# Third block of a four-block network on one Trainium2 core: normalization, rows and gate logits of two tiles placed directly behind the recurrence's work on them, with own room for the gate's matrix

## The chip, the core and the metric

The kernel runs on one core of a Trainium2 chip. A core has a matrix engine (PE, with its weight loads shown as PEld), a vector engine (DVE), an activation engine (ACT), GpSimd (POOL) and a sync engine (SP), which here does nothing but issue DMA transfers. Each engine works through its own queue in order, and they meet through semaphores. SBUF is the working memory with 128 partitions; PSUM is where PE writes and from which DVE and ACT read. The metric is device time in microseconds of one call, the median over runs; before the change it is 2966.4 us (three runs, 2960.71 to 2970.5).

## The reference

A residual stream x of 16 sequences of 64 tokens, 256 wide (1024 tokens, held as 8 tiles of 128 tokens), passes four blocks of cross-attention, a mixing layer and a feed-forward layer. The change touches the third block ("L2"): its linear recurrence and the routed experts behind it.

```python
x = x + _L2_xattn_ref(_layernorm(x), ctx_768, ...)          # 8 heads of 64 over 1024 keys
x = x + _L2_attn_ref(_layernorm(x), theta_log, nu_log, gamma_log, B_re, B_im, C_re, C_im, D)
x = x + _L2_ffn_ref(_layernorm(x), Wg, bg, W1, W2, W3)

def _L2_attn_ref(x, ...):                 # a complex linear recurrence along each sequence
    Bu = einsum('hd,bld->blh', B_norm, x)
    _, h = associative_scan(_binop, (Lam, Bu), axis=1)
    return einsum('oh,blh->blo', C, h).real + D * x

def _L2_ffn_ref(x, Wg, bg, W1, W2, W3):   # T = 1024 tokens, E = 8 experts, 2 of them per token
    gate_logits = xt @ Wg + bg
    top_v, top_i = top_k(gate_logits, 2)
    expert_label = one_hot(top_i, E).sum(axis=1)
    seq = cumsum(expert_label, axis=0) * expert_label
    valid = (seq > 0) & (seq <= 160)      # the first 160 tokens of each expert
    ...                                   # gather the rows of each expert
    h = silu(disp @ W1) * (disp @ W2)
    out = h @ W3
    ...                                   # weighted sum of a token's two outputs
```

The place of a token among those of its expert is a running sum over all 1024 tokens, so routing needs the logits of every tile.

## The kernel before

The layers run one after the other. `L2_xattn_attn` (line 1680) runs the cross-attention `heads64` (line 420) and the recurrence together: PE's order in it is the order in which the program text issues (a "manual schedule"), and the other engines are ordered by a scheduler.

`heads64` goes in 32 steps, four to a tile of 128 tokens. A step holds 13 us or more of PE work: transposes of the softmax of the step before (`keys_first`, L235), averages over keys (`misc<-ctx,pT`, from helper line 69), scores (L507), and every fourth step the output product (24 matmuls from L69). Between these it calls `breathe(0)` to `breathe(3)`; `breathe` is the recurrence's `go` (line 1800), which does nothing at place 3 and otherwise runs one piece of the current chunk. A chunk is two tiles, `chunk(k)` at line 1744, a generator cut in pieces by `yield`. Chunk k may start when the attention has finished tiles 2k and 2k+1 (`more`, line 1810). The pieces are, in order:

1. layer normalization of the two tiles on DVE and POOL into `os`;
2. four PE transposes of `os`, two evictions to `hTs` (one on DVE, one on ACT), and the D term on POOL;
3. eight matmul records into PSUM, scaled into `bu` on ACT;
4. products with cosine and sine and two scans on DVE and POOL; an empty piece follows;
5. eight matmul records back to 256 columns, added to the residual stream `xs` by DVE (L89).

So chunks 0, 1 and 2 run inside the attention's steps. Chunk 3 can start only after the last tile, when the attention has ended, and runs alone: `while lru.go(): pass`.

Then `L2_ffn` (line 1396) starts. `norm_x` (line 184) normalizes all eight tiles into `htok` (L170), transposes each (L179) and evicts to `hT` (lines 62 and 64, DVE and ACT in turn). `keep_row` (L1090) issues one DMA per tile, which writes the normalized rows to `hs` in HBM, from where experts gather them. `gate_logits` (line 1010) makes, for each tile, two matmuls with the gate's matrix and one with its bias row (the profile has two records for each matmul and one for each transpose): 128 x 8 outputs. DVE copies all logits to `lg` (L1404), and `route` (line 1092) computes top two, places and the table of tokens, on DVE with small matmuls. The gather of the first expert's rows (L1327, POOL's queue) waits for its result, `tokens` (L1411). Then eight experts run on PE.

Weights go through a ring of two slots; a "pack" takes a slot when its user two packs earlier is done, and one pack is loaded ahead. The gate's matrix and bias are a pack of their own (`pack_L2_gate`), between the recurrence's pack and expert 0's. PSUM tiles named `misc` come from two buffers in turn, so a third user waits for the eviction of the first. The tile `past` (line 1268) belongs to the block routing of the first and second block.

Of the kernel before, what the change touches and what calls it, by code (L numbers as in the profile page):

```python
# [11 lines left out]
F32 = mybir.dt.float32  # L12
# [3 lines left out]
ALU = mybir.AluOpType  # L16
# [3 lines left out]
B, S, D = 16, 64, 256  # L20
T = B * S
NT = T // 128
# [3 lines left out]
E = 8  # L26
# [16 lines left out]
class Net:  # L43
# [1208 lines left out]
    def block_experts(self, r, n_blocks, later=False):  # L1252

        nc = self.nc
        ps = self.misc([128, E])
# [9 lines left out]
        nc.vector.tensor_copy(n, end[:1, E - 1 :])  # L1265
        self.n_blocks = nc.values_load(n, min_val=0, max_val=n_blocks, skip_runtime_bounds_check_because="counted")
        shape = [128, n_blocks, E]
        past = self.lp.tile(shape, F32, name="past")
        nc.vector.tensor_tensor(
            past, self.steps[:, :n_blocks].unsqueeze(2).to_broadcast(shape),  # L1270
            end.unsqueeze(1).to_broadcast(shape), ALU.is_ge,
# [16 lines left out]
        ps = self.misc([128, n_blocks])  # L1288
# [14 lines left out]
        for m, to in zip(r.masks, r.at):  # L1303
            t = self.gate("back_t")
            nc.vector.tensor_tensor(t, r.place, first.unsqueeze(1).to_broadcast([128, NT, E]), ALU.add)
            nc.vector.tensor_tensor(t, t, m, ALU.mult)
            slot, _ = self.over_experts(t, ALU.add, "back_r")
# [75 lines left out]

        self.some_blocks(block, L1_FEW, L1_BLOCKS)

    def pack_L2_gate(self):
        self.slot()
        return self.load("L2f_Wg"), self.load_row("L2f_bg")

    def pack_L2_expert(self, e):  # L1390
        self.slot()
        return self.load("L2f_W1", e), self.load("L2f_W2", e), self.load("L2f_W3", e)
# [2 lines left out]

    def L2_ffn(self):
        nc = self.nc
        gw, gb = self.pack()
        self.norm_x()
        self.routed = r = self.route_setup(2)  # L1400
        for i in range(NT):
            self.keep_row(i)
        lg = self.gate("lg")
        nc.vector.tensor_copy(lg, self.gate_logits(gw, gb))  # L1404
        for _ in self.route(r, lg, 0, among_chosen=True):
            pass
        ps = self.misc([128, E, 2])
        cols = self.ident[:S, :S].rearrange("p (e n) -> p e n", e=E)[:, :, :2]
# [7 lines left out]
        for k, m in enumerate(r.masks):  # L1416
            t = self.gate("l2_t")
            nc.vector.tensor_tensor(t, late, m, ALU.mult)
            out, _ = self.over_experts(t, ALU.add, f"l2_late{k}")
            nc.vector.tensor_tensor(t, r.place, first.unsqueeze(1).to_broadcast([128, NT, E]), ALU.add)  # L1420
            nc.vector.tensor_tensor(t, t, m, ALU.mult)
            slot, _ = self.over_experts(t, ALU.add, f"l2_slot{k}")
# [6 lines left out]
        for e in range(E):  # L1429
# [10 lines left out]
            for v, (s0, n) in enumerate(L2_CUTS):  # L1440
                hb = self.lp.tile([n, D], F32, tag=f"hb{n}", bufs=2, name="hb")
                self.gather_rows(hb, self.hs, tokens[:n, e, v : v + 1])
                ps = self.misc([128, 2, 128])
# [4 lines left out]
            for m in range(8):  # L1448
                ps = self.lps.tile([128, 2, CAP], F32, tag="gu", bufs=2, name="gu")
# [7 lines left out]
            ps = self.lps.tile([128, 2, CAP], F32, tag="o", bufs=2, name="po")  # L1457
# [232 lines left out]
    def recurrence(self):  # L1690
        nc = self.nc
# [19 lines left out]
        def wrapped(x, n, name):  # L1711

            k = self.lp.tile([128, n], F32, name=f"{name}_k")
            nc.vector.tensor_scalar(k, x, 1.0 / two_pi, 12582912.0, ALU.mult, ALU.add)
            nc.vector.tensor_scalar(k, k, 12582912.0, None, ALU.subtract)
            y = self.lp.tile([128, n], F32, name=f"{name}_y")
            nc.vector.scalar_tensor_tensor(y, k, -hi, x, ALU.mult, ALU.add)
            nc.vector.scalar_tensor_tensor(y, k, -mid, y, ALU.mult, ALU.add)
            nc.vector.scalar_tensor_tensor(y, k, -lo, y, ALU.mult, ALU.add)
            nc.vector.tensor_scalar(y, y, PI_DOWN, -PI_DOWN, ALU.min, ALU.max)  # L1720
            return y

        phi = wrapped(theta, 1, "phi")
        ang = self.lp.tile([128, S], F32, name="ang")
        nc.vector.tensor_scalar(ang, self.steps, phi, None, ALU.mult)
# [15 lines left out]
        def flat(x):  # L1741
            return x.rearrange("p b s -> p (b s)")

        def chunk(k):
# [4 lines left out]
            for t in range(2):  # L1749
                x = self.xs[:, 2 * k + t, :]  # L1750
                mv, rs = self.norm_tile(x, 1e-5)
# [3 lines left out]
            hT = self.lp.tile([128, 2, CHUNK], F32, tag="hTs", name="hTs")  # L1755
            for t in range(2):
                self.evict(hT[:, :, t * 128 : (t + 1) * 128], self.transposed(os[t]))
                x = self.xs[:, 2 * k + t, :]
# [5 lines left out]
            for n, m in enumerate((br, bi)):  # L1764
                ps = self.misc([128, CHUNK])
# [27 lines left out]
            for t in range(2):  # L1793
                po = self.misc([128, D])
                at = slice(t * 128, (t + 1) * 128)
                self.mm(po, [(flat(hr)[:, at], cr), (flat(hn)[:, at], ci)])
                self.add_to_x(2 * k + t, po)
            yield

        def go(place=0):  # L1800
            if place == 3:
                return
            if s.work is None and s.next < NC and s.ready >= 2 * s.next + 2:
                s.work = chunk(s.next)
                s.next += 1
            if s.work is not None and next(s.work, s) is s:
                s.work = None
            return s.work is not None or s.next < NC
# [391 lines left out]
    def run(self, layers):  # L2200
        tc, nc, a = self.tc, self.nc, self.a
# [4 lines left out]
            "L1_attn": (self.L1_attn, [self.pack_L1_attn, self.pack_L1_boom]),  # L2206
            "L1_ffn": (self.L1_ffn, []),
            "L2_xattn_attn": (self.L2_xattn_attn, [lambda: self.pack_heads64("L2"), self.pack_L2_attn]),
            "L2_ffn": (self.L2_ffn, [self.pack_L2_gate] + [lambda e=e: self.pack_L2_expert(e) for e in range(E)]),
            "L3": (None, [lambda: self.pack_heads64("L3"), self.pack_L3_attn, self.pack_L3_ffn]),  # L2210
        }
        self.packs = [p for l in layers for p in plan[l][1]]
# [187 lines left out]
```

## Time and profile before

| what | value |
|---|---|
| median of three runs | 2966.4 us (2960.71 to 2970.5) |
| the profiled execution | 2962.24 us |
| span of its core in the profile | 2960.5 us |
| mean granted PE clock | 0.949 of full |
| PE / DVE / ACT busy share of the span | 91% / 49% / 35% |
| attention and recurrence of the third block, up to the last output product | ends at 1813.1 us |
| chunk 3 alone, to its last addition to `xs` | 1813.1 to 1830.6 us |
| transposes and gate matmuls of `L2_ffn` | 1830.7 to 1847.8 us |
| routing up to `tokens` | 1847.8 to 1864.6 us |
| first expert matmul | 1869.5 us |

The profiled execution took 2962.24 us, of which 2960.5 us are the span; the remaining 1.7 us lie around it. Rows of the timeline give the start, the duration, the engine, the line, the operation with output and inputs, the count of merged instructions, and in brackets the idle time before them and what ended it. The table of stretches gives, for each stretch, busy time and instruction count of PE, PEld, DVE, ACT and POOL, the granted PE clock as a share of full, the DMA share and the GB/s.

### The profile page before, as it was taken

What the parts mean: (1) busy time and instruction counts of PE and PEld (TensorE: products, weight loads), DVE (VectorE), ACT (ScalarE), POOL (GpSimd) and SP (SyncE); (2) the same over time, 40 slices, a digit from 0 to 9 for tenths busy, and PEclk for the clock granted to TensorE, in tenths of its full rate; (3) what the DMA queues carried; (4) which work ended last, traced back from release to release, by engine and by line L of the source; (5) the groups of instructions that cost most, each with busy time, mean ns of one, the idle gap of its engine ahead of it and who ended that gap; (6) DMA issues with size and microseconds to landing.
All of it is one profiled execution on the core that took longest, in us unless ns stands there. A gap on an engine that the chain in (4) does not pass through costs nothing. (4 is left out here: it accounts for less than half of the span.)

```text
span 2960.5 us, 42845 instructions
## 1 busy us (share of the span) xinstructions
PE 2687.8 (91%) x16972; PEld 1979.6 (67%) x16972; DVE 1462.2 (49%) x3117; ACT 1045.9 (35%) x2353; POOL 302.6 (10%) x407
## 2 busy tenths in 40 slices
PE   7887997999999898989999997899998898897899
PEld 3566784666666687857776776886766566665678
DVE  3655114666666643234444344324436656658581
ACT  2322122555555431223332331122335455455330
POOL 1111223000000112310101011201001000000000
PEclk9987998999999997989999997899999999998999
DMA  9603772110100115802111112551123122121210
GB/s 237 180 34 119 267 248 70 31 37 26 37 26 23 40 36 186 277 22 66 45 45 56 54 43 93 217 195 45 47 61 92 51 79 67 48 68 54 60 34 8
DMA packets 79222, 253.57 MB, mean 86 GB/s; under 512 B 15151, under 2 KB 26955, under 8 KB 69291
## 3 DMA queue, kind: packets, MB, share of 16 engines
q1 hardware_dynamic: 59562, 165.01, 18.0%
q0 software_dynamic: 13312, 80.28, 8.0%
q10 hardware_dynamic: 6144, 5.51, 0.5%
q8 instruction: 135, 2.21, 0.3%
q14 instruction: 69, 0.56, 0.1%
HBM read 233.80 MB, written 14.82 MB: 84 GB/s over the span
## 5 line engine op out<-in xcount | busy, mean ns | idle before, releaser
L223 DVE TENSOR_REDUCE nmx<-sc 128x1 f32<-128x1024 f32 x264 | 311.7, 1218 | 226.7 <-PE sc L507 135.2
L225 ACT ACTIVATE p<-sc,nmx 128x1024 f32<-128x1024 f32 x264 | 294.6, 1116 | 315.2 <-DVE nmx L223 314.5
L507 PE MATMUL sc<-ctxT,qp 128*128 128x512 f32 (+1 forms) x1024 | 357.7, 604 | 0.0
L507 PEld LDWEIGHTS sc<-ctxT,qp 128*128 128x128 f32 (+1 forms) x1024 | 139.5, 190 | 155.2 <-issue 153.0
L69 PE MATMUL halves<-ctx,pT 128*128 128x192 f32 x1024 | 191.0, 343 | 9.4 <-DVE xs L89 4.0
L69 PEld LDWEIGHTS halves<-ctx,pT 128*128 128x128 f32 x1024 | 178.3, 203 | 12.3 <-DVE xs L89 4.5
L69 PE MATMUL misc<-ctx,pT 128*128 128x192 f32 x1024 | 177.6, 327 | 0.5 <-DVE qT L472 0.5
L235 PE MATMUL ps_t<-ident,p 128*128 128x128 f32 x1088 | 146.8, 277 | 25.3 <-ACT p L225 17.6
L69 PEld LDWEIGHTS misc<-ctx,pT 128*128 128x128 f32 x1024 | 166.3, 191 | 2.2 <-DVE qT L472 1.0
L2010 ACT ACTIVATE da<-rep,al 128x252 f32<-128x252 f32 x256 | 114.7, 498 | 114.8 <-DVE x L2020 95.3
L237 ACT COPY pT<-ps_t 128x512 f32<-128x512 f32 x182 | 104.3, 585 | 139.3 <-PE ps_t L235 137.2
L235 PEld LDWEIGHTS ps_t<-ident,p 128*128 128x128 f32 x1088 | 126.7, 142 | 39.2 <-ACT p L225 22.5
L2020 DVE TENSOR_TENSOR_SCAN x<-da,x 128x512 f32<-128x512 f32 x128 | 151.9, 1211 | 1.9 <-ACT da L2010 1.4
L235 PE MATMUL misc<-ident,p 128*128 128x128 f32 x1024 | 138.3, 280 | 13.4 <-ACT p L225 6.3
L235 PEld LDWEIGHTS misc<-ident,p 128*128 128x128 f32 x1024 | 110.7, 141 | 39.8 <-ACT p L225 14.4
L160 POOL TENSOR_TENSOR ln_rs<-ln_ve,nhalf 128x1 f32<-128x1 f32 x80 | 45.1, 569 | 725.8 <-DVE ln_ve L158 676.0
L237 ACT COPY pT<-misc 128x512 f32<-128x512 f32 x128 | 75.0, 586 | 115.5 <-PE misc L235 115.1
L69 PE MATMUL ps_h<-r,w 128*128 128x256 f32 x512 | 115.3, 385 | 0.0
L69 PEld LDWEIGHTS ps_h<-r,w 128*128 128x128 f32 x512 | 97.8, 192 | 16.6 <-issue 2.9
L69 PE MATMUL gu<-dT,wa 128*128 128x128 f32 (+1 forms) x864 | 104.9, 280 | 3.7 <-ACT dT L64 2.4
L239 DVE COPY pT<-misc 128x512 f32<-128x512 f32 x128 | 88.2, 689 | 38.9 <-PE misc L235 28.2
L69 PEld LDWEIGHTS gu<-dT,wa 128*128 128x128 f32 (+1 forms) x864 | 98.4, 185 | 10.9 <-ACT dT L64 4.8
(477 smaller groups left out, 4482.5 us busy)
## 6 DMA issues: line engine op xcount, KB each, us to landing
ctx<-in_ctx SPq DMA_DIRECT2D x48, 768.0 KB, 4.3
ctxT<-in_ctxT SPq DMA_DIRECT2D x48, 512.0 KB, 3.8
w<-in_L2f_W SPq DMA_DIRECT2D x24, 1024.0 KB, 8.6
rep<-dus SPq DMA_DIRECT2D x256, 64.0 KB, 1.9
ctxT<-in_ctxT SPq DMA_DIRECT2D x16, 768.0 KB, 14.1
ctxT<-in_ctxT SPq DMA_DIRECT2D x96, 128.0 KB, 3.6
ys<-yb ACTq DMA_DIRECT2D x40, 128.0 KB, 5.4
bc_rep<-bcs SPq DMA_DIRECT2D x32, 128.0 KB, 3.2
```

The lines of the kernel that those rows point to most:

```text
L69: self.nc.tensor.matmul(out, lhsT, rhs, start=n == 0, stop=n == len(pairs) - 1)
L160: nc.gpsimd.tensor_tensor(rs, ve, self.nhalf, ALU.pow)
L223: self.nc.vector.tensor_reduce(nmx, sc, AX.X, ALU.max, negate=True)
L225: self.nc.scalar.activation(p, sc, AF.Exp, bias=nmx, accum_out=sums)
L235: self.nc.tensor.transpose(ps[:, u, :], p[:, at : at + 128], self.ident)
L237: self.nc.scalar.copy(pT[:, 4 * g : 4 * g + 4, :], ps)
L239: self.nc.vector.tensor_copy(pT[:, 0:4, :], ps)
L507: nc.tensor.matmul(sc[u][:, bass.ts(kh, 512)], qp[n][par][rows, h : h + 2, :].rearrange("p h q -> p (h q)"), ctx[0][rows, at], start=n == ...
L2010: nc.scalar.activation(da[:, g, :, 1:], now[j][:, 0, :].rearrange("p (b s) -> p b s", s=S)[:, :, 1:], AF.Exp, scale=al[:, col : col + 1],)
L2020: nc.vector.tensor_tensor_scan(flat, da.rearrange("p g b s -> p (g b s)"), flat, 0.0, ALU.mult, ALU.add)
```

## The change

Each chunk of the recurrence gets three more pieces behind its last one: normalization of its two tiles into `htok` with the row DMAs; transposes and evictions to `hT`; gate matmuls of these two tiles and a DVE copy of their logits. `L2_ffn` then starts from finished logits. The gate's matrix and bias leave the ring; they get tiles of their own and are loaded at the start of the recurrence, so that the ring has one pack less. `htok`, `hT` and `logits` are allocated at the start of the recurrence, and `past` moves to the room that `htok` uses. The numbers of matmuls, evictions and row DMAs stay; the one copy of 128 x 64 logits becomes four of 128 x 16.

```diff
--- before.py
+++ after.py
@@ -1265,7 +1265,7 @@
         nc.vector.tensor_copy(n, end[:1, E - 1 :])
         self.n_blocks = nc.values_load(n, min_val=0, max_val=n_blocks, skip_runtime_bounds_check_because="counted")
         shape = [128, n_blocks, E]
-        past = self.lp.tile(shape, F32, name="past")
+        past = self.act.tile(shape, F32, tag="htok", name="past")
         nc.vector.tensor_tensor(
             past, self.steps[:, :n_blocks].unsqueeze(2).to_broadcast(shape),
             end.unsqueeze(1).to_broadcast(shape), ALU.is_ge,
@@ -1383,10 +1383,6 @@
 
         self.some_blocks(block, L1_FEW, L1_BLOCKS)
 
-    def pack_L2_gate(self):
-        self.slot()
-        return self.load("L2f_Wg"), self.load_row("L2f_bg")
-
     def pack_L2_expert(self, e):
         self.slot()
         return self.load("L2f_W1", e), self.load("L2f_W2", e), self.load("L2f_W3", e)
@@ -1395,14 +1391,8 @@
 
     def L2_ffn(self):
         nc = self.nc
-        gw, gb = self.pack()
-        self.norm_x()
         self.routed = r = self.route_setup(2)
-        for i in range(NT):
-            self.keep_row(i)
-        lg = self.gate("lg")
-        nc.vector.tensor_copy(lg, self.gate_logits(gw, gb))
-        for _ in self.route(r, lg, 0, among_chosen=True):
+        for _ in self.route(r, self.logits, 0, among_chosen=True):
             pass
         ps = self.misc([128, E, 2])
         cols = self.ident[:S, :S].rearrange("p (e n) -> p e n", e=E)[:, :, :2]
@@ -1720,6 +1710,13 @@
             nc.vector.tensor_scalar(y, y, PI_DOWN, -PI_DOWN, ALU.min, ALU.max)
             return y
 
+        self.htok = self.act.tile([128, NT, D], F32, tag="htok", name="htok")
+        self.hT = self.act.tile([128, 2, T], F32, tag="hT", name="hT")
+        self.logits = self.act.tile([128, NT, E], F32, name="logits")
+        gw = self.lp.tile([128, 2, E], F32, name="gw")
+        nc.sync.dma_start(gw, self.a["L2f_Wg"])
+        gb = self.lp.tile([1, E], F32, name="gb")
+        nc.sync.dma_start(gb, self.a["L2f_bg"])
         phi = wrapped(theta, 1, "phi")
         ang = self.lp.tile([128, S], F32, name="ang")
         nc.vector.tensor_scalar(ang, self.steps, phi, None, ALU.mult)
@@ -1795,6 +1792,25 @@
                 at = slice(t * 128, (t + 1) * 128)
                 self.mm(po, [(flat(hr)[:, at], cr), (flat(hn)[:, at], ci)])
                 self.add_to_x(2 * k + t, po)
+            yield
+
+            tiles = range(2 * k, 2 * k + 2)
+            for i in tiles:
+                x = self.xs[:, i, :]
+                mv, rs = self.norm_tile(x, 1e-5)
+                nc.vector.tensor_scalar(self.htok[:, i, :], x, mv[:, 0:1], rs, ALU.subtract, ALU.mult)
+                self.keep_row(i)
+            yield
+            for i in tiles:
+                self.evict(self.hT[:, :, i * 128 : (i + 1) * 128], self.transposed(self.htok[:, i, :]))
+            yield
+            ps = self.misc([128, 2, E])
+            for t, i in enumerate(tiles):
+                self.mm(
+                    ps[:, t, :],
+                    [(self.hT[:, c, i * 128 : (i + 1) * 128], gw[:, c, :]) for c in range(2)] + [(self.ones[:1, :], gb)],
+                )
+            nc.vector.tensor_copy(self.logits[:, 2 * k : 2 * k + 2, :], ps)
             yield
 
         def go(place=0):
@@ -2206,7 +2222,7 @@
             "L1_attn": (self.L1_attn, [self.pack_L1_attn, self.pack_L1_boom]),
             "L1_ffn": (self.L1_ffn, []),
             "L2_xattn_attn": (self.L2_xattn_attn, [lambda: self.pack_heads64("L2"), self.pack_L2_attn]),
-            "L2_ffn": (self.L2_ffn, [self.pack_L2_gate] + [lambda e=e: self.pack_L2_expert(e) for e in range(E)]),
+            "L2_ffn": (self.L2_ffn, [lambda e=e: self.pack_L2_expert(e) for e in range(E)]),
             "L3": (None, [lambda: self.pack_heads64("L3"), self.pack_L3_attn, self.pack_L3_ffn]),
         }
         self.packs = [p for l in layers for p in plan[l][1]]
```

In the program built from it, PE's order has, three times inside the attention (once for each of chunks 0 to 2): four transposes of `htok` between the averages and the second `keys_first` of a step, then behind that `keys_first` twelve gate records, then scores. On SP the two row DMAs of a chunk stand ahead of the next fetch of keys, and the loads of `gw` and `gb` ahead of the stage's first fetch. On DVE the normalization stands directly behind the two additions to `xs`. Behind chunk 3, the order is: four transposes, twelve gate records, routing.

## Prediction

> **What bounds the kernel now.** I read the page first: PE is busy for nine tenths of the span. The change lives in one stage, so I then read the table of stretches around it.
>
> ```profile
> PE 2687.8 (91%) x16972; PEld 1979.6 (67%) x16972; DVE 1462.2 (49%) x3117; ACT 1045.9 (35%) x2353; POOL 302.6 (10%) x407
> ...
> 1500.00:1550.00 50.00, 49.29 (x283) 37.01 (x282) 21.45 (x50) 15.48 (x41) 4.29 (x6) 1.00 0.12 35
> ...
> 1813.00:1831.00 18.00, 7.67 (x24) 4.91 (x23) 14.36 (x46) 1.32 (x3) 8.63 (x13) 0.65 0.13 44
> 1831.00:1848.00 17.00, 16.02 (x64) 13.79 (x62) 3.01 (x12) 1.49 (x4) 1.07 (x2) 0.50 0.53 200
> 1848.00:1868.00 20.00, 8.63 (x39) 7.45 (x40) 15.46 (x93) 0.26 (x1) 2.51 (x3) 0.59 0.70 272
> ```
>
> Two regimes. Inside the attention PE works 49.3 of 50 us at the full clock (1.00): whatever PE is given there lengthens the stage. Behind it everything is serial: chunk 3 is bound by DVE and POOL (1813 to 1831), then PE transposes and gates at half clock (0.50), then DVE routes. PE work moved from the second regime to the first is therefore not hidden; it is paid again, but at the full clock. The timeline shows both prices.
>
> ```profile
> 1835.89 1.02 PE L69 MATMUL misc<-w,hT 128*128 128x8 f32 x4
> 1836.84 0.59 PE L69 MATMUL misc<-w,ones 1*128 1x8 f32 x2
> 1837.37 1.02 PE L69 MATMUL misc<-w,hT 128*128 128x8 f32 x4
> ...
> 1847.79 0.23 DVE L1404 COPY lg<-misc 128x64 f32<-128x64 f32 x1 [11.95 <-PE misc L69]
> ```
> ```profile
> 1101.95 0.51 PE L69 MATMUL misc<-w,hTs 128*128 128x8 f32 x4
> 1102.39 0.38 PE L69 MATMUL misc<-w,ones 1*128 1x8 f32 x2
> 1102.70 0.61 PE L69 MATMUL misc<-w,hTs 128*128 128x8 f32 x4
> 1103.25 0.38 PE L69 MATMUL misc<-w,ones 1*128 1x8 f32 x2
> 1103.56 0.61 PE L69 MATMUL misc<-w,hTs 128*128 128x8 f32 x4
> 1104.10 0.38 PE L69 MATMUL misc<-w,ones 1*128 1x8 f32 x2
> 1104.41 0.61 PE L69 MATMUL misc<-w,hTs 128*128 128x8 f32 x4
> ```
>
> From start to start, a tile's gate costs 1.48 us behind the recurrence (1835.89 to 1837.37). The same shapes in the second block's router, at the full clock, cost 0.75, 0.86 and 0.85 us: 0.82 on average. DVE idles 11.95 us ahead of the logits copy, so the gate sets the end here.
>
> **Part 1, what leaves the serial stretch.** (a) Gate matmuls of six tiles: 6 x 1.48 = 8.9 us. (b) Transposes. Before, the last addition to `xs` starts at 1830.22 and the gate at 1835.89, 5.7 us later, since 16 transposes (5.2 us, at two PSUM buffers) go between. After, only tiles 6 and 7 are left and their normalization is the path: from that addition 0.4 for it, 0.4 statistics of tile 7, then by DVE's order tile 6's small operations, power (POOL 0.55) and `htok` (0.41) and tile 7's after it, some 1.5 more and again 0.8: `htok` 7 is ready 3.1 us after the addition's start, its transposes take 0.6 at half clock, so the gate starts at 3.8. That gives 1.9 (1.2 to 2.4). PE loses some cover here: the transposes of tiles 0 to 5 had run beside the normalization of 6 and 7. (c) Chunk 3 shares DVE with the normalization of tiles 0 to 5, six times 0.42 + 0.17 + 0.14 + 0.41 = 6.8 us, which leaves. But most of it fills gaps. Chunk 0, undisturbed, goes from the end of its second `bu` (1447.84) to the end of its last DVE operation (1453.25) in 5.4 us; chunk 3 needs from 1820.46 to 1826.63, 6.2. That is 0.8, and 0.3 more because `os` of tile 7 need not wait behind foreign statistics (1.93 us in chunk 0, 2.26 in chunk 3): 1.1 (0.8 to 1.7). (d) Two small DVE copies (0.14 each) move behind the logits: +0.15. Sum: 8.9 + 1.9 + 1.1 - 0.15 = 11.7 us less, bounds 10.7 to 12.9.
>
> **Part 2, what three chunks pay inside the attention.** Per chunk PE gets four transposes (two rows of two in 0.22 each: 0.44), and twelve gate records (two tiles at 0.82: 1.64). A wait comes with them: the second pair of transposes needs the `misc` buffer of the averages, whose eviction is DVE then ACT. The recurrence's own transposes stand at this very place and show it:
>
> ```profile
> 1572.27 2.77 PE L69 MATMUL misc<-ctx,pT 128*128 128x192 f32 x16
> 1574.87 0.38 PE L179 MATMUL misc<-ident,os 128*128 128x128 f32 x2
> 1576.78 0.44 PE L179 MATMUL misc<-ident,os 128*128 128x128 f32 x2 [1.53 <-ACT on L522]
> ```
>
> In the three chunks this wait is 0.74, 1.53 and 0.46 us. The steps confirm a whole price: the step with these transposes and eight matmuls (1.73) lasts, from scores to scores, 24.33, 25.12 and 23.71 us, against 21.29 for its kind without a chunk (for the third 20.62, as it lacks 0.67 of another transposing piece): 3.0, 3.8 and 3.1 for 2.2 of PE work. With the gate's 1.64 in place of 1.73 I take 3.0 per chunk, 9.0 in all. Low: no wait, 0.44 + 1.5 = 1.9 per chunk, 5.8. High: the dearest step and the 0.3 by which a following step was longer, 4.1 per chunk, 12.4.
>
> **Part 3, what I cost at nothing.** DVE's normalization behind the additions: after 1464.35 DVE has 4.10 us idle before the `qp` copies (1468.87). Two tiles and the one of the attention that is put behind them cost three times 1.14 with three powers of 0.55 in between, ending near 1468.6. If that cover fails, `qp` and then the row maxima (1469.75) are late; the softmax that PE wants at 1473.37 is done at 1472.3, so one more microsecond is free, and each beyond costs itself, thrice. ACT gets one copy of 0.37 per chunk ahead of a `pT` copy, in the step's price. On SP two row DMAs stand ahead of a key fetch that was issued at 1467.78 for scores at 1513; they delay it by one or two microseconds out of over forty. `gw` and `gb` are two issues of 0.33 behind a DMA at 1235.74, and PE wants keys at 1288. `past` waits for row DMAs, the last issued at 262.05 with 1.8 to land, and runs at 275.71. Expert 0's weights start at 1813 instead of 1830.25, expert 1's near 1830 instead of 1847.78; PE has its first expert matmul at 1869.48 and waits there for gathered rows, not weights, so nothing is gained or lost; uncovered, a late 1 MB load costs its 8.6 us. Routing and experts shift as they are.
>
> **Sum.** -11.7 + 9.0 = -2.7 us. The profiled execution of 2962.24 (span 2960.5 and 1.7 around) becomes 2959.5; its 4.2 below the median of 2966.4 is spread between runs, so the median is forecast at 2963.7. Bounds: -12.9 + 5.8 = -7.1 to -10.7 + 12.4 = +1.7, that is 2959.3 to 2968.1. A difference under 0.3%, 8.9 us, is about what a measurement of this kernel can't tell from none.
>
> **A rule against the change.** In the second block, four gated tiles at the full clock were followed by a slower clock:
>
> ```profile
> 1102.00:1104.00 2.00, 2.00 (x17) 1.92 (x15) 0.00 (x0) 1.83 (x3) 0.00 (x0) 1.00 0.00 0
> 1104.00:1106.00 2.00, 2.00 (x11) 1.89 (x11) 0.38 (x2) 0.29 (x1) 0.00 (x0) 0.74 0.00 0
> 1106.00:1108.00 2.00, 2.00 (x6) 1.57 (x5) 1.46 (x9) 1.51 (x2) 0.00 (x0) 0.50 0.00 0
> 1108.00:1110.00 2.00, 2.00 (x9) 1.72 (x9) 0.61 (x6) 0.00 (x0) 0.00 (x0) 0.91 0.00 0
> ```
>
> PE was busy throughout, and yet lost 0.52 + 1.0 + 0.18 = 1.7 us of full clock. The first block's gate, eight records at 124.89, kept 1.00 in the stretches 123 to 130. Two tiles lie between. In the new place transposes, a wait, eight more transposes and the gate stand in a row, 0.44 + 0.8 + 0.87 + 1.64 = 3.75 us, about as long as those 3.5. The Trainium skill (TensorE: Matmul & The Clock Gate, Parts 1 and 4) says that the clock is halved after a window of about 3.4 us without enough activity and that transposes don't count as activity. By that rule each chunk could lose 1.7 and the sum is +2.4; by the first block's row it stays -2.7. The recurrence's own run of transposes and waiting, 1574.87 to 1577.93 (3.1 us), kept the clock, so I take the row.
>
> **The rivals.**
> - *PE has room.* The pieces slip into PE's pauses in the attention and cost nothing: 2966.4 - 11.7 = 2954.7. For it: steps with waits exist. Against it: 0.7 us of pause in 50. Chance 0.10.
> - *The clock drops.* Place: the scores behind each gate piece; price 1.7 a chunk; it decides from two drops (2 x 1.7 > 2.7), and with three the time is 2966.4 + 2.4 = 2968.8, slower than before. For it the 1104 to 1110 rows, against it those at 123 to 130. Chance 0.12.
> - *It doesn't shorten the serial stretch.* If the experts waited for weights, or routing for something other than logits, the 11.7 would be lost: 2966.4 + 9.0 = 2975.4. Against it: the 11.95 us of DVE idle that end with PE. Chance 0.04.
>
> **How the numbers follow.** The forecast has 0.72; 0.02 is left for what I don't see. The predicted time is 2963.7. The range starts from its own 2959.3 to 2968.1, is widened by some 2 us for a median of three runs that spread over 9.8, and takes in the clock rival: 2957 to 2970. Faster by over 0.3% (under 2957.5): nearly all of the first rival and a small part of the forecast, 0.13. Slower by over 0.3% (over 2975.3): half of the third rival, a part of the second with dearer waits, and the unseen, 0.05. Within: 0.82.
>
> **What would show it.** From the last output product (1813.1) to the logits copy before routing: 34.7 us now, 23.0 forecast. From the first scores to that product: 9.0 longer, in three steps of 3.0. At the htok transposes a wait of 0.5 to 1.5 for the averages' eviction. Gate tiles at 0.8 us and a clock of 1.00 behind them. I am wrong if those steps grow by under 1.9 (first rival) or over 4.1, if the clock column falls there, or if the stretch from logits to first expert matmul changes from its 21.7 us.

## The result and the profile after

| | before | after |
|---|---|---|
| median | 2964.33 us (14 runs, 2959.17 to 2970.5) | 2959.41 us (14 runs, 2955.82 to 2966.73) |
| profiled execution; span | 2962.24; 2960.5 us | 2958.03; 2956.3 us |
| attention, from scores behind the first tile to the last output product | 431.9 us | 441.3 us |
| from there to the logits copy | 34.5 us | 21.6 us |
| logits copy to first expert matmul | 21.7 us | 21.6 us |

The ratio is 0.9988 with a 95% interval of 0.998 to 0.9995 (the two medians alone give 0.9983): a gain of 0.12%, within the 0.3% that the prediction counted as no change. The forecast was 2963.7 (2957 to 2970). The attention is measured from the first row of scores behind the first tile's output product (1381.39 before, 1380.90 after; the block's very first scores start at 1288.23 and 1288.02) to DVE's first addition to `xs` behind the last output product (1813.31 and 1822.24); all stage times below use these two marks, also where a text says "from first scores" (from the very first scores the attention is 9.1 us longer than before, from the mark 9.4). Its stages sum to 3.4 us less than before (466.4 and 463.0).

The page's line of engines and the table of stretches, for after. Columns as before: length, busy time and count of PE, PEld, DVE, ACT, POOL, granted PE clock, DMA share, GB/s.

```profile
PE 2678.9 (91%) x16972; PEld 1971.3 (67%) x16972; DVE 1463.3 (49%) x3120; ACT 1046.2 (35%) x2353; POOL 303.4 (10%) x407
```
```profile
1500.00:1550.00 50.00, 49.29 (x283) 37.02 (x282) 21.86 (x51) 15.19 (x38) 4.29 (x6) 1.00 0.14 45
1822.00:1840.00 18.00, 7.25 (x23) 4.59 (x21) 9.39 (x25) 1.32 (x3) 6.81 (x9) 0.76 0.54 198
1840.00:1844.00 4.00, 3.38 (x15) 3.14 (x14) 0.88 (x4) 0.37 (x1) 0.00 (x0) 0.50 0.94 338
1844.00:1864.00 20.00, 8.62 (x39) 7.27 (x40) 15.56 (x95) 0.26 (x1) 2.45 (x3) 0.59 0.49 196
```

PE's record count is the same as before; only places have changed. The stretch of transposes and gates behind chunk 3, 17 us of PE at half clock before, is 4 us. The timeline of after shows its gate:

```profile
1840.96 0.87 PE L69 MATMUL misc<-gw,hT 128*128 128x8 f32 x4
1841.77 0.59 PE L69 MATMUL misc<-gb,ones 1*128 1x8 f32 x2
1842.29 1.02 PE L69 MATMUL misc<-gw,hT 128*128 128x8 f32 x4
1843.24 0.59 PE L69 MATMUL misc<-gb,ones 1*128 1x8 f32 x2
1843.87 0.18 DVE L1813 COPY logits<-misc 128x16 f32<-128x16 f32 x1 [3.11 <-PE misc L69]
```

Two tiles instead of eight, and DVE's idle time ahead of the logits is 3.11 us instead of 11.95. In the attention the three new pieces look like this (PE's timeline of after; the first row is the scores behind the first chunk's piece, the others are the third chunk's piece):

```profile
1480.79 5.62 PE L507 MATMUL sc<-ctxT,qp 128*128 128x512 f32 x16
...
1745.43 0.38 PE L179 MATMUL misc<-ident,htok 128*128 128x128 f32 x2
1746.27 0.44 PE L179 MATMUL misc<-ident,htok 128*128 128x128 f32 x2 [0.46 <-ACT hT L64]
1746.55 1.04 PE L235 MATMUL ps_t<-ident,p 128*128 128x128 f32 x8
1747.42 0.51 PE L69 MATMUL misc<-gw,hT 128*128 128x8 f32 x4
1747.86 0.38 PE L69 MATMUL misc<-gb,ones 1*128 1x8 f32 x2
1748.17 0.61 PE L69 MATMUL misc<-gw,hT 128*128 128x8 f32 x4
1748.72 0.38 PE L69 MATMUL misc<-gb,ones 1*128 1x8 f32 x2
1749.03 7.32 PE L507 MATMUL sc<-ctxT,qp 128*128 128x512 f32 x16
```

The piece is as forecast, 0.75 and 0.86 us a tile and a wait of 0.46 (0.70 in the other two chunks). But the scores behind the third piece take 7.32 us, those behind the first and second 5.62: the clock fell once. The question that is left is why once, and not never or three times.

### The profile page after: what moved, and what is told of

The parts are those of the page before. It is cut to its first block, busy times and chain, and to the rows that moved or that the text cites. A ratio compares the mean times of both kernels' runs of the same rounds, so it can differ in the third digit from the quotient of the medians.

```text
span 2956.3 us, 42844 instructions
## 1 busy us (share of the span) xinstructions
PE 2678.9 (91%) x16972; PEld 1971.3 (67%) x16972; DVE 1463.3 (49%) x3120; ACT 1046.2 (35%) x2353; POOL 303.4 (10%) x407
```

## The experiments

Each row below is one profiled execution. "Chunk 3" is the time from the start of the first addition to `xs` behind the last output product to the start of the last addition of chunk 3, "to the gate" from there to the first gate matmul, "gate" from there to the logits. The last column names the chunks whose new pieces were followed by a fallen clock.

| kernel | attention | chunk 3 | to the gate | gate | sum behind the attention | clock falls in the attention |
|---|---|---|---|---|---|---|
| before | 431.92 | 16.91 | 5.67 | 11.90 | 34.48 | none |
| after | 441.34 | 15.03 | 3.69 | 2.91 | 21.63 | third |
| E1 own room only | 431.45 | 16.92 | 5.68 | 11.89 | 34.49 | none |
| E2 normalization and rows | 430.93 | 17.08 | 5.67 | 11.90 | 34.65 | none |
| E3 and transposes | 434.51 | 15.04 | 3.71 | 11.74 | 30.49 | none |
| E4 after, gate one step later | 439.55 | 16.49 | 3.68 | 2.91 | 23.08 | none |
| E5 after, gate twice | 451.39 | 17.08 | 3.68 | 2.91 | 23.67 | all three |
| E6 after, one buffer for transposes | 437.12 | 16.43 | 4.17 | 3.06 | 23.66 | none |
| E7 after again | 441.20 | 15.41 | 3.69 | 2.91 | 22.01 | second |
| E8 one buffer for all, bias on DVE | 433.27 | 16.92 | 4.16 | 1.92 | 23.00 | none |
| E9 after again, timed | 441.36 | 15.04 | 3.54 | 2.64 | 21.22 | third |
| E10 E8, two buffers in chunk 3 | 433.36 | 17.08 | 3.69 | 1.76 | 22.53 | none |
| E11 E10 with filling matmuls | 433.36 | 13.24 | 3.55 | 1.27 | 18.06 | none |

Whole times of single executions say little here: the attention's first mark lies anywhere between 1379.9 and 1388.4 us in these kernels, and between 1380.5 and 1383.3 us in three executions of the same one, so the verdicts rest on the stages. The single whole times were 2962.32 (E1), 2965.42 (E2), 2957.01 (E3) and 2962.12 (E4), with 2960.0 for before beside them, and 2969.39 (E5), 2960.60 (E6) and 2959.91 us (E7). E2's and E4's are against their expectations (faster than before by 2 to 5, and faster than after by 1.7): E2's first mark (1388.35) is already 7 us later than that of before.

### E1 to E4: one part after the other

E1 takes the pieces out again and keeps the gate's tiles:

```diff
-            tiles = range(2 * k, 2 * k + 2)
-            for i in tiles:
...
 def L2_ffn(self):
+        self.norm_x()
         self.routed = r = self.route_setup(2)
+        for i in range(NT):
+            self.keep_row(i)
+        nc.vector.tensor_copy(self.logits, self.gate_logits(self.gw, self.gb))
```

> Only the gate's own room is kept: its matrix and bias are loaded when the recurrence starts, the ring has one pack less, past shares htok's room; all work stands in the order of the kernel before. My theory (the room alone is worth nothing): as before, 34.7 us from the last output product to the logits copy and 21.7 from there to the first expert matmul, run within 3 us of the kernel before beside it. Rival (expert 0's weights, which can load 17 us earlier, or the shorter ring, give part of the gain): the stretch from logits to first expert matmul, or the experts behind it, become shorter than 21.7 or than before by a microsecond or more.

Measured: 34.49 us behind the attention, 21.60 from the logits to the first expert matmul (21.69 before); one run of 2962.32. The room and the earlier weights are worth nothing; the rival falls.

E2 leaves the normalization and the row DMAs in the chunks, and transposes and gates go back:

```diff
                 self.keep_row(i)
-            for i in tiles:
-                self.evict(self.hT[:, :, i * 128 : (i + 1) * 128], self.transposed(self.htok[:, i, :]))
-            yield
-            ps = self.misc([128, 2, E])
...
 def L2_ffn(self):
+        for i in range(NT):
+            self.evict(self.hT[:, :, i * 128 : (i + 1) * 128], self.transposed(self.htok[:, i, :]))
+        nc.vector.tensor_copy(self.logits, self.gate_logits(self.gw, self.gb))
```

> Normalization and row DMAs stay in the chunks, all transposes and gate matmuls go back behind chunk 3. My theory: DVE's part is hidden in the attention, so PE's steps there grow by nothing and lose what os waits less (0.9 + 0.1 us) where the attention's own normalization is put behind htok's; behind it the stretch from the last output product to the logits copy is 34.7 - 1.9 (chunk 3 has DVE for itself) - 0 to 2.0 (transposes of tiles 0 to 5 need not wait for their normalization) = 30.8 to 32.8 us. So attention -0 to -1.0 against before, run 2 to 5 us faster than before. Rival (the normalization is not hidden in the attention, three powers on POOL and six tiles on DVE make qp and the softmax late): steps with the normalization grow by 0.5 us or more each.

Measured: attention 430.93, 0.5 less than E1 and 1.0 less than before, so the normalization is hidden there. Behind it the expectation missed: 34.65 us instead of 30.8 to 32.8. E2's PE timeline shows the two reasons.

```profile
1823.06 3.78 PE L69 MATMUL misc<-hTs,w 128*128 128x256 f32 x8 [0.46 <-ACT hTs L64]
...
1836.83 3.53 PE L179 MATMUL misc<-ident,htok 128*128 128x128 f32 x12 [0.51 <-DVE xs L89]
1840.82 1.12 PE L179 MATMUL misc<-ident,htok 128*128 128x128 f32 x4 [0.46 <-ACT hT L64]
```

All sixteen transposes start behind the last addition, although six tiles had been normalized long before; and the recurrence's eight matmuls take 3.78 us, against 1.99 in after, because the clock fell there. So normalizing early gained nothing for the transposes. What it gains in chunk 3 was lost to the clock here: with the 15.04 us that chunk 3 takes in E3, the sum would be 32.6 (an estimate), inside the expectation.

E3 leaves the transposes in the chunks too:

```diff
-            yield
-            ps = self.misc([128, 2, E])
...
 def L2_ffn(self):
+        nc.vector.tensor_copy(self.logits, self.gate_logits(self.gw, self.gb))
```

> Normalization, rows and transposes stay in the chunks; the gate matmuls of all eight tiles go back behind chunk 3. My theory: against after, the attention's three long steps lose 1.64 us each (4.9) and the slower scores of the third chunk (7.32 instead of 5.62) disappear, as no gate matmuls stand ahead of them; behind it the gate's 6 x 1.48 = 8.9 us come back at half clock, 21.8 + 8.9 = 30.7 us from last output product to logits copy. Sum +4.0 - 1.7 = +2.3 us against after. Rival A (the drop comes from the transposes and their wait): one of the scores behind a htok piece still takes over 7 us. Rival B (gate matmuls were hidden in the attention): its steps lose under 0.5 us each.

Measured: attention 434.51, where 441.34 - 4.9 - 1.7 = 434.7 was expected; 30.49 us behind it (30.7). No scores row over 5.6 us. Rival B falls; rival A too, as far as one execution can show it.

E4 moves the gate one step away from the transposes:

```diff
                 self.evict(self.hT[:, :, i * 128 : (i + 1) * 128], self.transposed(self.htok[:, i, :]))
+            for _ in range(3):
+                yield
             yield
             ps = self.misc([128, 2, E])
```

> The gate matmuls of a chunk come one step later than in after, so that htok's transposes, their wait and the gate no longer stand in one run. My theory (the slower clock in the third chunk came from a run of 3.75 us without large matmuls): all three scores behind a gate piece take 5.6 us, the clock stays 1.00 there, attention 1.7 us shorter than in after, the stretch behind it unchanged at 21.8; run -1.7 against after. Rival (the gate matmuls alone bring the drop, wherever they stand, or it comes by chance): a scores row of over 7 us at one or more of the three new places.

Measured: the three scores rows behind a gate take 5.62 us, attention 439.55, 1.8 less than after. Behind it 23.08 instead of the 21.8 expected: the recurrence's matmuls in chunk 3 took 3.44 us instead of 1.99. The clock fell at 1828.57, 0.4 us behind their start; in after it fell only behind them, at 1831.18. As after itself had only one slow row of three, one execution without any can't exclude chance, the second half of the rival; the grid, below, does.

Together these make a ladder for the attention: 431.45 (room), 430.93 with normalization (-0.5), 434.51 with transposes (+3.58, 1.19 a chunk), 439.55 with gates (+5.04, 1.68 a chunk), 441.34 with one fall of the clock (+1.8).

### E5, E7, E9: where the clock falls

In each trace the granted clock changes only at times that differ by whole multiples of 3.413 us (after has 66 records of it, 3.41, 6.83, 10.24, 13.65 us long and so on). With the grid of one execution fixed by its other changes, after's pieces can be cut along it. The table of stretches of after: for each piece the stretch of the grid that holds most of it and the next one, and a third behind the third chunk's:

```profile
1476.20:1479.61 3.41, 2.71 (x22) 2.44 (x20) 1.41 (x3) 0.92 (x3) 0.00 (x0) 1.00 0.00 0
1479.61:1483.02 3.41, 3.41 (x14) 2.16 (x14) 0.20 (x2) 0.36 (x1) 0.00 (x0) 1.00 0.00 0
1612.73:1616.14 3.41, 3.41 (x24) 3.09 (x25) 0.87 (x2) 0.96 (x2) 0.00 (x0) 1.00 0.02 5
1616.14:1619.55 3.41, 3.41 (x9) 1.25 (x10) 0.00 (x0) 0.00 (x0) 0.00 (x0) 1.00 0.00 0
1745.85:1749.26 3.41, 2.99 (x23) 2.91 (x24) 1.44 (x4) 1.19 (x3) 0.00 (x0) 1.00 0.00 0
1749.26:1752.67 3.41, 3.41 (x5) 1.35 (x5) 0.05 (x1) 0.00 (x0) 0.00 (x0) 0.50 0.00 0
1752.67:1756.08 3.41, 3.41 (x12) 1.14 (x11) 0.52 (x1) 0.00 (x0) 0.00 (x0) 1.00 0.00 0
```

The third piece, 1745.43 to 1749.03, fills the stretch 1745.85 to 1749.26 but for 0.23 us of scores, and the next stretch is granted 0.50, whole, then 1.00 again: half of 3.41 is 1.7 us, the price. The boundary at 1479.61 cuts the first piece in two; 0.92 us of averages lie in its stretch. The second shares its stretch with 0.72 us of scores. Both keep 1.00. PE's busy column says nothing of it: 2.71 of 3.41 kept the clock, 2.99 lost it.

E7 and E9 are after, unaltered.

> The changed kernel once more, unaltered. My theory (whether the clock falls at a gate piece depends on where the grid of 3.41 us lies against the program in this execution): each of the three scores rows takes 5.6 or up to 7.3 us, a slow one with a chance of about a quarter, and a slow one exactly where a whole stretch of the grid lies between the averages and the scores; attention 439.6 + 1.7 for each. Rival (the third chunk's place in the program decides): the third row takes 7.3 again and the first two 5.6.

Measured (PE's timeline of E7, the scores behind the three pieces, then the stretches of its grid around the second):

```profile
1480.34 5.62 PE L507 MATMUL sc<-ctxT,qp 128*128 128x512 f32 x16
...
1615.15 7.04 PE L507 MATMUL sc<-ctxT,qp 128*128 128x512 f32 x16
...
1750.16 5.62 PE L507 MATMUL sc<-ctxT,qp 128*128 128x512 f32 x16
```
```profile
1611.23:1614.64 3.41, 2.71 (x24) 2.41 (x22) 1.44 (x3) 1.27 (x3) 0.00 (x0) 1.00 0.02 5
1614.64:1618.05 3.41, 3.41 (x7) 1.83 (x7) 0.17 (x1) 0.00 (x0) 0.00 (x0) 0.50 0.00 0
```

The same program, another chunk: the place in the program does not decide, the grid does. Here the second piece (1611.11 to 1615.15) covers 1611.23 to 1614.64 whole. In E9, below, it was the third again, with 0.20 us of scores in its stretch.

E5 lengthens the piece:

```diff
-            for t, i in enumerate(tiles):
+            for t, i in [*enumerate(tiles)] * (2 if k < 3 else 1):
                 self.mm(
```

> The gate matmuls of chunks 0 to 2 are issued twice, with the same result. My theory (a gate tile's 0.82 us is paid in full at the full clock): three times 1.64 = 4.9 us more in the attention, from first scores to last output product 439.6 (after without its slow scores) + 4.9 = 444.5 us. To this comes the clock: it changes on a fixed grid of 3.41 us, and falls when one whole stretch of the grid holds next to no large matmul; the run without large matmuls is now 5.4 us long, so a fall is likelier than not at each of the three pieces (about 0.7 each), at up to 1.7 us each. Rival A (the gate's matmuls count as work for the clock): no fall at any piece. Rival B (gate work slips into pauses): under 2 us more in all.

Measured (PE's timeline of E5, the scores behind the three pieces):

```profile
1483.62 7.32 PE L507 MATMUL sc<-ctxT,qp 128*128 128x512 f32 x16
...
1622.37 8.12 PE L507 MATMUL sc<-ctxT,qp 128*128 128x512 f32 x16
...
1760.20 7.32 PE L507 MATMUL sc<-ctxT,qp 128*128 128x512 f32 x16
```

The gate pieces grew by 1.71 us each at the full clock (in the first chunk 1480.30 to 1483.62 is 3.32, 1.61 in after), 5.1 in all, and the clock fell at all three. Two falls cost 1.7 as expected; the second cost 3.2 (2.5 in the scores, 0.7 in the gate matmuls ahead of them), as two stretches in a row were granted 0.50. The table of stretches of E5 shows it; the first of these stretches is PE busy throughout, with transposes and gate matmuls alone:

```profile
1617.21:1620.62 3.41, 3.41 (x28) 3.31 (x28) 0.69 (x1) 0.96 (x2) 0.00 (x0) 1.00 0.02 5
1620.62:1624.03 3.41, 3.41 (x10) 2.52 (x11) 0.17 (x1) 0.00 (x0) 0.00 (x0) 0.50 0.00 0
1624.03:1627.45 3.42, 3.42 (x5) 1.35 (x4) 0.00 (x0) 0.00 (x0) 0.00 (x0) 0.50 0.00 0
```

In sum, 439.55 + 5.1 + 6.6 = 451.3 are expected from these parts, and 451.39 were measured. Both rivals fall: gate matmuls are paid in full, and for the clock they hardly count.

### E6, E8, E10: without the wait and the bias

E6 writes the four transposes into one PSUM buffer:

```diff
-            for i in tiles:
-                self.evict(self.hT[:, :, i * 128 : (i + 1) * 128], self.transposed(self.htok[:, i, :]))
+            ps = self.misc([128, 4, 128])
+            for n in range(4):
+                nc.tensor.transpose(
+                    ps[:, n, :], self.htok[:, tiles[n // 2], (n % 2) * 128 : (n % 2 + 1) * 128], self.ident
+                )
+            for t, i in enumerate(tiles):
+                self.evict(self.hT[:, :, i * 128 : (i + 1) * 128], ps[:, 2 * t : 2 * t + 2, :])
```

> The four htok transposes of a chunk write one PSUM buffer instead of two, so that none of them waits for the averages' eviction. My theory: the waits of 0.70, 0.70 and 0.46 us go, attention 439.6 - 1.9 = 437.7 us, and no clock falls at the pieces, as the run without large matmuls is 3.1 us, less than one stretch of the grid. Rival (the wait moves to the next user of the buffers, the keys' transposes or the gate): attention as in after without its slow scores, 439.6.

Measured: attention 437.12, 2.4 less than E4. PE's timeline of E6 has one row of four transposes with no wait, and no fall:

```profile
1479.59 0.60 PE L1806 MATMUL misc<-ident,htok 128*128 128x128 f32 x4
1480.03 1.04 PE L235 MATMUL ps_t<-ident,p 128*128 128x128 f32 x8
```

The rival falls. In chunk 3 the same edit costs 0.5 us (4.17 to the gate instead of 3.69).

E8 does the same for `os` too, loads the bias into all 128 partitions and replaces its matmuls; the last part of the edit is:

```diff
-                    [(self.hT[:, c, i * 128 : (i + 1) * 128], gw[:, c, :]) for c in range(2)] + [(self.ones[:1, :], gb)],
+                    [(self.hT[:, c, i * 128 : (i + 1) * 128], gw[:, c, :]) for c in range(2)],
                 )
-            nc.vector.tensor_copy(self.logits[:, 2 * k : 2 * k + 2, :], ps)
+            nc.vector.tensor_tensor(
+                self.logits[:, 2 * k : 2 * k + 2, :], ps, gb.unsqueeze(1).to_broadcast([128, 2, E]), ALU.add
+            )
```

> One PSUM buffer for the four transposes of os and of htok alike, and the bias added by DVE on the way out of PSUM instead of by two matmul records per tile. My theory: against after without its slow scores the attention loses the htok waits (1.9 us), the os waits (1.7) and the bias records (3 x 0.65 = 1.9): 434.1 us; behind it two bias records at half clock, 1.2 us: 20.5 us from last output product to logits copy where the clock holds in chunk 3, up to 1.8 more where it falls. Sum against the kernel before: +2.2 - 14.0 = -11.8 us, about 2952.5, ratio 0.996. Rival (the waits move on to the next users): attention 437.7, ratio 0.997 to 0.998.

Measured: attention 433.27, gate behind it 1.92 us; the attention won what was expected. Behind it 23.0 us missed the 20.5, and the 22.3 with a fallen clock: the recurrence's matmuls took 3.63 us instead of 1.99, and the shared buffer cost 0.5, as E6 showed. Median 2954.14 (11 runs) against 2961.46, ratio 0.9973, interval 0.996 to 0.9986: short of the expected 0.996 and in the rival's band, but the rival's attention of 437.7 was not seen.

E10 gives each tile its own buffer in chunk 3:

```diff
+    def turned(self, k, two):
+        if k == 3:
+            return [self.transposed(h) for h in two]
+        ps = self.misc([128, 4, 128])
...
```

> As the version with one PSUM buffer and the bias on DVE, but in chunk 3, which has no averages ahead of it, each tile's transposes keep a buffer of their own. My theory (in chunk 3 the shared buffer made the first tile's eviction wait for the second tile's transposes): attention 433.3 us as there; in chunk 3 0.5 us less between the last addition to the residual stream and the gate (3.7 instead of 4.16) and 0.4 less ahead of the recurrence's matmuls; 20.6 us from last output product to logits copy where the clock holds, 22.1 where it falls. Rival (4.16 came from the slow clock): 4.1 again.

Measured: 3.69 us to the gate, so the shared buffer was the cause of 4.16. The 0.4 us ahead of the recurrence's matmuls were not seen: they start 3.78 us behind the first addition (3.77 in E8), and the clock fell before them. Ratio 0.9959, interval 0.9944 to 0.9974 (5 runs).

> The changed kernel unaltered, timed beside the two that follow on the same chip. My theory: attention 439.6 us plus 1.7 for each gate piece where the clock falls; from last output product to logits copy 21.6 us plus up to 1.8 where it falls in chunk 3; ratio to the kernel before 0.998 to 1.000. Rival (the ratio of 0.9988 came from the clock's luck alone): 1.000 or above.

E9, on the same chip: ratio 0.9987, interval 0.9977 to 0.9997, 2961.35 against 2965.99. The gain of after is small and real; its rival falls.

### E11: the clock behind the attention

```diff
+        def fill(n):
+            ps = self.misc([128, CHUNK])
+            for _ in range(n):
+                nc.tensor.matmul(ps, self.ident, decay, start=True, stop=True)
+
+            if k == 3:
+                fill(6)
...
+            if k == 3:
+                fill(10)
...
+            if k == 3:
+                fill(6)
```

> As the version before it, with 22 matmuls of 128x256 that nobody reads put into PE's idle time in chunk 3: 6 ahead of the transposes of os, 10 between the recurrence's matmuls, 6 ahead of htok's transposes. My theory (behind the attention PE's work costs twice as much only because PE has been idle, and keeping it at work keeps the clock): clock 1.00 up to the gate; the recurrence's matmuls back take 1.9 us instead of 3.75, the gate 1.0 instead of 1.9; from last output product to logits copy 17.5 to 18.5 us, 2 to 4 less than without. Rival A (the added matmuls stand in front of real ones and delay them): 20.6 or more. Rival B (the clock falls all the same): gate tiles at half clock, 0.59 us for two records of a bias or 1.0 for four of the gate.

Measured, PE's timeline of E10 (first) and of E11 (second), from the recurrence's matmuls to the gate:

```profile
1825.54 3.78 PE L69 MATMUL misc<-hTs,w 128*128 128x256 f32 x8 [0.46 <-ACT hTs L64]
1835.05 1.19 PE L69 MATMUL misc<-w,ur 128*128 128x256 f32 x2 [5.73 <-DVE ur L1795]
...
1842.53 1.73 PE L69 MATMUL misc<-gw,hT 128*128 128x8 f32 x8
```
```profile
1821.21 1.99 PE L69 MATMUL misc<-hTs,w 128*128 128x256 f32 x8 [0.46 <-ACT hTs L64]
1823.04 4.51 PE L1752 MATMUL misc<-later,ident 128*128 128x256 f32 x20
1828.94 0.67 PE L69 MATMUL misc<-w,ur 128*128 128x256 f32 x2 [1.39 <-DVE ur L1804]
...
1830.74 2.75 PE L1752 MATMUL misc<-later,ident 128*128 128x256 f32 x12
...
1834.49 1.24 PE L69 MATMUL misc<-gw,hT 128*128 128x8 f32 x8
```

From the matmuls to the gate 13.28 us instead of 16.99, 18.06 us behind the attention instead of 22.53, and the clock 1.00 in every stretch of the grid from 1817.81 to 1838.29. The ten fillers end before DVE is done (1.39 us of idle are left ahead of `ur`), and the others delay nothing that counts: the recurrence's matmuls start 3.51 us behind the first addition (3.78 in E10), the gate 3.55 behind the last (3.69). The gate took 1.27 us, not the expected 1.0. Both rivals fall. E10's profiled execution was one with a fallen clock in chunk 3; with the 15.03 us that chunk 3 takes in after, its sum would be 20.5 (an estimate), so the filling wins 2.4 to 4.5 us. Ratio 0.9942, interval 0.9926 to 0.9958 (6 runs, median 2947.53 against 2965.99): with E8's and E10's edits it beats before and after by a measurable amount.

## Why the prediction was right, step by step

The time came out 4.3 us below the forecast, inside its range. Of this 2.1 are luck of the starting point, as before has a median of 2964.33 over 14 runs, not the 2966.4 of three that the forecast started from; the difference, forecast at -2.7, was -3.4 in the stages and -4.9 between the medians. The account holds in the main: work moved from a half-clock stretch into a full one, 12.85 us won behind the attention and 9.42 paid in it, where -11.7 and +9.0 were forecast.

- *(a), the gate of six tiles.* Forecast 8.9, measured 11.90 - 2.91 = 9.0; E3 against after gives 8.8. Right.
- *(b), transposes.* Forecast 1.9, measured 5.67 - 3.69 = 2.0. E2 and E3 show which part brings it: the transposes (5.67 to 3.71), not the normalization (5.67 in E2).
- *(c), chunk 3.* Forecast 1.1 (0.8 to 1.7), measured 1.9: mis-sized. The 0.3 us ahead of the recurrence's matmuls were right (0.4), and so was chunk 0 as the undisturbed case: from the end of the second `bu` to DVE's end it is 5.4 us there and 5.35 in chunk 3 of after. What failed is the other side, 6.2 from 1820.46: that `bu` came late, as those matmuls ran at a fallen clock (2.69 us), so the interval left out most of the delay. DVE came to `ur` (line 1773 before, 1770 after) 1.5 us after the first `bu` had ended (1818.90), in E1 too; in after at once. With the matmuls at 1.99 us in both, the interval is 6.87 in E1, 1.5 more than in after, and PE's wait ahead of `ur` is 7.25 against 5.73. In before and E1 this delay covered a slower clock as well (2.69 us for those matmuls and 16.91 for chunk 3 in before, 1.99 and 16.92 in E1). In after nothing covers it: 15.03 where the clock holds, 17.08 where it falls (E5). So, against these two executions, (c) lies between 1.9 and nothing. ACT's and DVE's timelines of before (first) and after (second):

```profile
1818.43 0.47 ACT L1768 ACTIVATE bu<-misc,ex 128x256 f32<-128x256 f32 x1 [1.28 <-PE misc L69]
1820.43 0.41 DVE L1773 TENSOR_TENSOR ur<-bu,cos 128x256 f32<-128x256 f32 x1
```
```profile
1826.99 0.47 ACT L1765 ACTIVATE bu<-misc,ex 128x256 f32<-128x256 f32 x1 [1.28 <-PE misc L69]
1827.50 0.42 DVE L1770 TENSOR_TENSOR ur<-bu,cos 128x256 f32<-128x256 f32 x1 [2.69 <-ACT bu L1765]
```

- *(d), two copies.* Forecast +0.15; from the logits copy to the next operation on them it is 0.23 us after and 0.26 before. Nothing.
- *Part 2, 3.0 a chunk.* The steps grew by 2.96, 2.97 and 2.73 us. By the ladder: transposes with their wait 1.19 a chunk (1.36 forecast), the gate 1.68 (1.64). The sum of 9.42 comes near 9.0 by errors of opposite sign, which is luck: +1.8 for a fall of the clock, -0.5 for the transposes, -1.0 for a wait of the recurrence that became shorter, shown below.
- *Part 3, costed at nothing.* Right for rows, room and weights (E1: 21.60 from logits to experts). The normalization was not nothing but a small gain (E2: -0.5).

The shorter wait is seen on DVE. The timelines of before (first) and after (second), around the averages' eviction `on` (L521) in the second chunk:

```profile
1573.62 0.48 DVE L1336 SCALAR_TENSOR_TENSOR xs<-back,route_g,xs 128x256 f32<-128x256 f32 x1 [0.96 <-DMA back<-ys,route_at]
...
1575.64 0.41 DVE L460 TENSOR_SCALAR o<-xs,ln_mv,ln_rs 128x256 f32<-128x256 f32 x1 [0.66 <-POOL ln_rs L160]
1575.97 0.41 DVE L521 TENSOR_SCALAR on<-misc,av_r 128x192 f32<-128x192 f32 x1
```
```profile
1575.58 0.48 DVE L1336 SCALAR_TENSOR_TENSOR xs<-back,route_g,xs 128x256 f32<-128x256 f32 x1 [0.42 <-DMA back<-ys,route_at]
...
1577.56 0.42 DVE L521 TENSOR_SCALAR on<-misc,av_r 128x192 f32<-128x192 f32 x1 [1.37 <-PE misc L69]
```

Before, the attention's own normalization `o` stood ahead of `on` and waited for POOL, and an addition of the second block's expert rows (L1336) ahead of both waited 0.96 us for its DMA; PE's second pair of `os` transposes then waited 1.53 us. In E1, with DVE's order unchanged, the wait for that DMA was 0.56 us and PE's 1.13: this 0.4 us of the gain is not the normalization's, and nothing shows that it is the change's at all. With the new normalization in the chunk, the scheduler put `o` behind it (1601.87 in after), and PE's wait is 0.64, in E2 as in after: another 0.5.

- *The rule against the change.* The forecast weighed two answers for all three chunks, none or 1.7 each. The truth is between: one piece of three in after, in E7 and in E9. The mechanism of the rival was right, and its price; what failed was to treat it as a property of the program. The rows I took for "kept" said little: the first block's run from transposes to scores lasts 1.2 us (124.61 to 125.77) and the recurrence's 3.1, too short to fill a stretch of 3.41 wherever it lies, while the new piece lasts 3.84 (1476.95 to 1480.79), of which 3.68, 3.67 and 3.44 us in the three chunks lie between the end of the averages and the scores. The Trainium skill (TensorE: Matmul & The Clock Gate, Part 1) says that the window of 3413 ns is free-running and that its phase against a kernel differs by run; the traces agree (3.413 us, another phase in each execution), and that sentence was the one to use. If a stretch falls that holds under about 0.5 us of scores or averages, at its start or at its end, a gap of 3.60 us (the mean) makes the clock fall in an estimated (3.60 - 3.41 + 2 x 0.5) / 3.41 = 0.35 of the phases. Three of nine did.

The rival "PE has room" falls with E5 and the ladder, "it doesn't shorten the serial stretch" with the 12.85 us.

## What to carry to other kernels

Price moved PE work at the clock of both places: a gate tile cost 1.48 us where the clock was granted 0.50 and 0.82 where it was granted 1.00, so moving it was worth less than its old price and more than nothing. Before moving work into a busy stretch, try to make the idle one cheaper: 22 matmuls that nobody reads, put where PE waits, won 4.5 us between the profiled executions of E10 and E11 (22.53 to 18.06), and an estimated 2.4 against an E10 whose clock holds in chunk 3; the whole move won 3.4. Keep pieces of transposes and narrow matmuls well under one 3.41 us stretch in a row, or put them in different steps: by the 0.70 us that held, under an estimated 3.41 - 0.70 = 2.7 us no phase of the clock's grid should hurt. E4's gaps between averages and scores, 2.1 and 2.3 us, are below it; E6's, 2.75 to 2.82, kept the clock in all three places, but in one execution only.

## What the runs showed of the hardware that was not expected

- The clock's two values last whole multiples of 3.413 us in every trace, with one phase per execution. In the attention a stretch of the grid that was granted 1.00 was followed by 0.50 when it held 0.00 to 0.47 us of matmuls of 128 columns or more (not counting transposes; six cases), and by 1.00 with 0.70 or more. One that was granted 0.50 held 1.66 us of scores and was followed by 0.50 again (E5, 1620.62 to 1624.03). In chunk 3, where PE idles for the rest of the stretch, stretches at 1.00 with as much as 1.00 to 1.15 still fell and those with 1.24 to 1.35 held: transposes and gate matmuls seem to count for a little, which no run measured by itself.
- A busy PE does not hold the clock: 3.41 of 3.41 us busy with transposes and gate matmuls was followed by 0.50 (E5, 1617.21 to 1620.62).
- Part of the spread behind the attention is the same lottery: the recurrence's eight matmuls in chunk 3 took 1.99, 2.69, 2.76, 3.38, 3.44, 3.63 or 3.78 us in these kernels, with the same eight records; in E4 and after, above, the place of the grid's boundary made the difference. How much of the 8.5 us by which the attention's first mark moves has this cause stays open.
